# A two-layer attention kernel on one core: the order of score and value runs, of two projections, of some loads and of a few sums is changed

## The chip, the core and the metric

The kernel runs on one core of a Trainium2 chip. A core has five engines with a queue of instructions each: TensorE (in the profile PE, its weight loads PEld), which multiplies matrices and writes to PSUM; VectorE (DVE); ScalarE (ACT); GpSimd (POOL); and SyncE (SP), which here only issues DMA transfers, as GpSimd does too. Each queue is worked in the order written; engines wait for each other by semaphores. SBUF holds the working data, PSUM the sums of the matmuls, in eight banks of 128 x 512 float32. The metric is the device time of one execution in microseconds; lower is better.

## The reference

All is float32. The input x is 8 x 512 x 32 x 32: 8 batches of 512 channels and 1024 positions (tokens).

Layer 0, for each batch: a layer norm over the 512 channels of each token, then `q`, `k`, `v` = xn @ W.T + b, split into 8 heads of 64 channels; `softmax(q k^T / 8) v` in each head; then

```python
out = out @ Wo.T + bo + residual
```

where `residual` is x itself.

Layer 1, for each batch, on the result: a group norm (32 groups of 16 channels), `q`, `k`, `v` from three 512 x 512 matrices, one head of 512 channels:

```python
logits = jnp.einsum('bcn,bcm->bnm', q, k) * scale
attn = jax.nn.softmax(logits, axis=-1)
o = jnp.einsum('bnm,bcm->bcn', attn, v)
out = jnp.einsum('oc,bcn->bon', wp, o) + bp[None, :, None]
return x + out.reshape(B, C, H, W)
```

## The kernel before

**Work per batch.** `fast_path` takes the batches one after the other and both layers of a batch together. (A second path, for scores that overflow, is compiled but not entered.) For a batch: values and queries of layer 0; attention of layer 0; the key projection of the next batch's layer 0, first unit; output projection with residual; group norm, with the second unit of the keys beside it; layer 1 (query-key product `qa` with wq and wk multiplied into one matrix, scores, values with wv and wp multiplied into one, output). The order of TensorE, VectorE, ScalarE and GpSimd is the order in which the Python code emits the instructions (`manual_schedule`), SP's order too.

**Seven products.** Every 512 x 512 by 512 x 1024 product is done on 2 x 2 blocks with seven block products in place of eight. `STEPS` lists them: two operands, one of three PSUM sums `x`, `y`, `z`, and whether the sum is opened or continued. Block sums of the weights are called S1 to S4, those of the data T1 to T4 (`add_operand`, VectorE, 128 x 1024 each). A `Product` is half of such a multiplication (a unit, r = 0 or 1). `step` emits one block product (four full-array matmul records of 512 columns) and then the work due with it: a copy of the sum out of PSUM (`copy`, by a `shift` function that adds bias or residual) and additions into the result (`out`). After step 4 the block (1,1) is formed from `x` and `y`; step 6 continues `y` and so waits until VectorE has read it.

**Side work.** `later` puts small pieces on a list; `tick` emits one, once per step of a product and once per key chunk of the values; `until` empties the list as far as needed. Layer norm of a later batch (`LayerNorm.queue`), operand sums and the softmax sums are spread over the TensorE work in this way.

**Attention of layer 0.** A `Pair` is two heads (128 channels) against half of the queries (512); there are 8 pairs a batch, i = 0 to 7. `scores` makes 8 tiles, one for each 128 keys: the two heads' matmuls use 64 rows of the array each and run side by side into the two banks of one wide PSUM tile (`wide_psum`, pool of three), ScalarE takes the exp of the whole tile into SBUF (`p`), and VectorE adds the tiles up into `sum`. `values` multiplies with the values, each head in 64 columns of the array, into one single bank (`bank`, pool of two), and ScalarE copies that to `o`. The loop runs one pair ahead: scores 0, rest of the queries, scores 1, values 0, scores 2, values 1, ... scores 7, values 6, values 7. A float32 matmul of the code appears as two records in the profile, so scores of a pair are 32 records in 16 steps of two.

**Softmax sums.** Two pairs make a `PairSums`. After a pair's scores GpSimd's DMA queue halves and folds `sum` (lines 529, 533); VectorE then transposes, reduces and inverts it (`invert_folded`, `invert_sums`, lines 537 to 538 and 774 to 778), ScalarE makes eight small copies (line 864), VectorE spreads them (line 523) and scales `o` (line 873). The inverse is emitted at tile m = 4 of a later score run in the first half of a batch, and as side work in the second. In the last batch the last two pairs are summed by matmuls with ones instead (`product`, tile `den`).

**Residual.** In the output projection (`project_out`) the `shift` function issues the DMA for the residual `xr` when the sum is ready to be copied, and VectorE adds it (line 889). `x1_away`, `w_a`, `w_m` are other DMAs of that stage in SP's queue.

**The opening.** Weights are loaded, wq and wk (and wv and wp) of layer 1 multiplied into one, layer norm of batch 0 done in pieces (`norm(n)` emits n of them). `complete("k", wk_now)` emits the key weights' block sums on GpSimd (line 218) and stores them for later batches (line 211).

**Pools.** SBUF tiles of 128 x 1024 come from a pool of 46, those of 128 x 512 from a pool of 9. A tile that takes a slot waits for the last reader of the slot's previous tile.

The loop that the change turns around:

```python
next_scores()
q_last.rest()
for i in range(HEADS):
    p = pairs[i]
    if i + 1 < HEADS:
        next_scores()
    ...
    p.values(scaled=(i == HEADS - 1 and not more))
```

Of the kernel before, what the change touches and what calls it, by code (L numbers as in the profile page):

```python
# [15 lines left out]
ALU = mybir.AluOpType  # L16
# [4 lines left out]
P = 128  # L21
# [40 lines left out]
]  # L62
BLOCK_OF = {1: (0, 0), 4: (1, 1), 5: (1, 0), 6: (0, 1)}
SLOTS = ["11", "12", "22", "S1", "S2", "S3", "S4"]


@with_exitstack
def fast_path(ctx: ExitStack, tc: tile.TileContext, x: bass.AP, vecs: dict, weights: dict, out: bass.AP,
# [174 lines left out]

    def complete(n, w):

        sums_of_blocks(nc.gpsimd, w)
        save_w(n, w)

    def complete_later(n, w):
# [4 lines left out]

    wk_now, wv_now = first_w("k"), first_w("v")
    wo = first_w("o")
    wq_now = first_w("q")
    nc.sync.dma_start(out=bq1_row, in_=vecs["bq1"].rearrange("(a c) -> a c", a=1).to_broadcast((P, C)))
# [70 lines left out]
    class Product:  # L329
# [4 lines left out]
        def __init__(self, tag, a, b, part, shift, dest, banks, after=None):  # L334
            self.tag, self.a, self.b, self.part, self.shift, self.dest = tag, a, b, part, shift, dest
            self.banks = banks
            self.after = after or (lambda i, k: None)
            self.behind = []
            self.ahead = None
            self.in_place = False  # L340
            self.pieces = 1
            self.at_once = False
            self.led = []
            self.last = None
            self.done = 0
# [7 lines left out]
        def copy(self, which):  # L353
            u = half_tile(f"u{which}_{self.tag}")
            self.shift(u, self.x, which)
            return u
# [12 lines left out]
        def step(self, n=1):  # L369
            for _ in range(n):  # L370
# [4 lines left out]
                self.open(to, opens)  # L375
                if self.ahead and i + 1 in BLOCK_OF:
                    self.ahead(*BLOCK_OF[i + 1])
                if i in self.led:
# [133 lines left out]
    def add_operands(b):  # L512
        later(*(lambda n=n: add_operand(b, n) for n in ("T1", "T2", "T3", "T4")))

# [266 lines left out]
    class Pair:  # L781


        def __init__(self, b, hf, c, qt, kt, vt, ot):
            self.tag = f"{b}_{hf}_{c}"
            self.hf, self.c, self.vt = hf, c, vt
            self.q = qt[c // 2, hf][:, c % 2, :]
            self.k = [kt[c // 2, k][:, c % 2, :] for k in range(NH)]
            self.p = {}
            self.sum = self.rden = None  # L790
            if c % 2 == 0:
                ot[c // 2, hf] = block(f"o_{self.tag}")
            self.o = ot[c // 2, hf][:, c % 2, :]

        def scores(self, ms):
            for m in ms:
                s = wide_psum(f"s_{self.tag}_{m}")
                for i in range(2):
                    r = slice(i * D, (i + 1) * D)
                    nc.tensor.matmul(s[:, ts(i, HB)], self.k[m // 4][r, ts(m % 4, P)], self.q[r, :],  # L800
                                     start=True, stop=True)
                p = big_tile(f"p_{self.tag}_{m}")
                nc.scalar.activation(p, s, AF.Exp, scale=1.0 / float(D) ** 0.5)  # L803
                self.p[m] = p
# [9 lines left out]
        def values(self, scaled):  # L814
            acc = bank(f"acc_{self.tag}")
            for m in range(NM):
# [10 lines left out]
    class PairSums:  # L827
# [23 lines left out]
        def product(self):  # L851

            self.den = bank(f"den_{self.tag}")
            for k in range(4):
# [20 lines left out]
    def project_out(b, w, ot, stats):  # L875
# [4 lines left out]
        def unit(r):  # L880
            def dest(i, k):
                return x1[i, k][:, r, :]

            def shift(u, ps, which):
                i, k = which
                oc = 2 * i + r
                xr = half_tile(f"xr_{b}_{k}_{oc}")
                nc.sync.dma_start(out=xr, in_=x[b, ts(oc, P), ts(k, HB)])
                nc.vector.scalar_tensor_tensor(u, ps, bo[:, oc : oc + 1], xr, ALU.add, ALU.add)

            def after(i, k):
                later(lambda: nc.vector.bn_stats(stats[:, 2 * i + r, k, :], dest(i, k)))

            return Product(f"out_{b}_{r}", w, ot, channel_part(r), make_shift(shift, True), dest,
                           banks_of(f"out_{b}", r, shared, own="x"), after)
        return [unit(r) for r in range(2)], x1


    class Whole:
# [96 lines left out]
        def values(self, v):  # L996
# [4 lines left out]
            def unit(r):  # L1001
# [6 lines left out]

                def ahead(i, k):
                    if u.last and (i, k) == (0, 1):  # L1010
                        return
                    xr = xr_of[i, k] = half_tile(f"x1r_{b}_{k}_{2 * i + r}")
                    nc.sync.dma_start(out=xr, in_=self.x1[i, k][:, ts(r, HB)])
# [59 lines left out]
    with tc.manual_schedule(engines=ORDERED):  # L1073
# [9 lines left out]

        complete("k", wk_now)
        norm(5)
# [8 lines left out]
        bm_columns.rows(lambda c: [(slice(0, C), wp[c])])  # L1094
        product(wa, nq, nk, "a", 1)
        bm_columns.columns()
        norm(100)
        for k in range(NH):
            for j in range(2):
# [14 lines left out]

        for n, w in (("v", wv_now), ("q", wq_now), ("o", wo), ("a", wa), ("m", wm)):
            complete_later(n, w)
# [7 lines left out]

        def next_values_and_queries(b, wv, wq, ln):

            units, v = project_v(f"v{b}", wv, hb)
            if b == 0:
# [3 lines left out]
            for u in units:  # L1132
                u.rest()
            units, q = project(f"q{b}", wq, bias_of("bq0"), hb, True)
            for u in units:
                u.pieces = 1 if b else 2
            units[0].step(1)
            if ln:
                ln.waiting = False
            units[0].rest()  # L1140
            return v, q, units[1]

        vts, qt, q_last = next_values_and_queries(0, wv_now, wq_now, ln)
        for b in range(B):
# [12 lines left out]

            next_scores()
            q_last.rest()
            for i in range(HEADS):  # L1160
                p = pairs[i]
                if i + 1 < HEADS:
                    next_scores()
                if i < 2 and more:
# [6 lines left out]
                if i == 7 and more:  # L1171
                    hb = operands(ln.result())
                    add_operands(hb)
                p.values(scaled=(i == HEADS - 1 and not more))
                sums = groups[i // 2]
# [3 lines left out]
                elif i % 2 == 1 and sums.folded:  # L1179
# [4 lines left out]
                    else:  # L1184
                        later(nothing, nothing, sums.invert_folded)
                    later(sums.copies, *(lambda s=sums, f=f, n=n: f(s, n) for f in (PairSums.rows, PairSums.scale)
                                         for n in range(2)))
            if more:
                k_units, kn = project(f"k{b + 1}", wk_next, bias_of("bk0"), hb, True)
                k_units[0].rest()  # L1190
            ob = operands(ot)
            o_units, x1 = project_out(b, wo_now, ob, stats)
            o_units[0].step(1)
# [59 lines left out]
            if more:  # L1253
                wv_next = load_w("v", b + 1)
            o_units = whole.values(vm)
# [15 lines left out]
            if more:  # L1271
                wq_next = load_w("q", b + 1)
            if more:
                kt = {ik: block(f"k{b + 1}_again_{ik[0]}{ik[1]}") for ik in kn_away}
                for ik, d in kn_away.items():
                    nc.sync.dma_start(out=wide(kt[ik]), in_=d)
                vts, qt, q_last = next_values_and_queries(b + 1, wv_next, wq_next, ln)

# [383 lines left out]
```

## Time and profile before

| | us |
|---|---|
| median of three runs | 2914.44 |
| lowest and highest run | 2912.37, 2914.49 |
| the profiled execution, time | 2912.76 |
| the profiled execution, span | 2911.0 |

| engine | busy, us | share of the span |
|---|---|---|
| PE | 2889.0 | 99% |
| PEld | 1373.0 | 47% |
| DVE | 1794.9 | 62% |
| ACT | 1055.5 | 36% |
| POOL | 352.7 | 12% |

The granted clock of TensorE is 0.999 of full speed over the span. The lines below show, for a group of equal instructions: start in us from the span's start, time from the first one's start to the last one's end, engine, line of the code, operation, tiles written and read, shape, count, and in brackets how long the engine was idle before and what ended that. Where matmuls follow each other, their recorded lengths overlap (0.59 us each, 0.43 apart), so stretches of TensorE are read from start to start. A line of the chain shows start, length and what ran.

### The profile page before, as it was taken

The page shows a single profiled execution, that of the slowest core. Times are in us where ns is not written, and L with a number is a line of the kernel's source. Part 1 is how long each engine was busy: PE and PEld are TensorE (multiplying, and loading weights), DVE is VectorE, ACT ScalarE, POOL GpSimd, SP SyncE. Part 2 cuts the span into 40 slices and gives each one's busy share as a digit, 9 for nine tenths or more (in the row PEclk, how much of TensorE's full clock was granted, in tenths as well). Part 3 has the DMA queues.
Part 4 walks back from the last instruction along what each step waited for, and adds up shares of the span by engine and source line. Part 5 has one row for each costly group of instructions (what it writes and reads, how often), then busy time and mean ns, then how long its engine had stood idle before and what let it go on. Part 6 is the DMA issues. An engine that isn't in the chain of part 4 may idle for free.

```text
span 2911.0 us, 27160 instructions
## 1 busy us (share of the span) xinstructions
PE 2889.0 (99%) x9695; PEld 1373.0 (47%) x9695; DVE 1794.9 (62%) x2320; ACT 1055.5 (36%) x1724; POOL 352.7 (12%) x511
## 2 busy tenths in 40 slices
PE   9999999999999999999999999999999999999999
PEld 4534455345543455434553345533455334553345
DVE  6677465774657655676556765577556675537744
ACT  3462314612156122651226412264223632126221
POOL 3020011200112011120111201021010210002000
PEclk9999999999999999999999999999999999999999
DMA  8124153341623326233252333423243331412302
GB/s 303 59 62 144 37 152 83 63 145 36 179 52 63 141 54 170 48 65 134 66 158 51 69 127 85 140 55 77 115 119 105 64 112 71 127 32 61 110 8 66
DMA packets 110127, 277.15 MB, mean 95 GB/s; under 512 B 16304, under 2 KB 20704, under 8 KB 109984
## 3 DMA queue, kind: packets, MB, share of 16 engines
q1 hardware_dynamic: 81760, 204.51, 20.2%
q0 software_dynamic: 28128, 70.81, 13.1%
q8 instruction: 78, 1.28, 0.2%
q14 instruction: 65, 0.53, 0.1%
q10 hardware_dynamic: 96, 0.02, 0.0%
HBM read 168.85 MB, written 59.24 MB: 78 GB/s over the span
## 4 chain that ended last, share of the span: by engine, by line
PE 96%; DVE 2%; DMA 1%; issue 0%; ACT 0%; SPq 0%; DVEq 0%; ACTq 0%
PE s L800 15%; PE acc L818 15%; PE x_o L456 6%; PE x_s L448 6%; PE y_s L448 4%; PE z_s L448 4%; PE z_o L456 4%; PE y_o L456 4%; PE x_k L431 3%; PE x_q L431 3%; PE x_v L440 3%; PE x_vm L440 3%; PE x_qa L431 3%; PE x_out L431 2%; PE y_k L431 2%; PE z_qa L431 2%
## 5 line engine op out<-in xcount | busy, mean ns | idle before, releaser
L803 ACT ACTIVATE p<-s 128x1024 f32<-128x1024 f32 x512 | 476.0, 1052 | 76.8 <-PE s L800 76.8
L809 DVE TENSOR_TENSOR sum<-sum,p 128x1024 f32<-128x1024 f32 x384 | 470.3, 1225 | 39.8 <-DVE sum L809 1.4
L818 PE MATMUL acc<-p,v 128*64 128x512 f32 x2048 | 452.0, 595 | 1.3 <-ACT o L822 1.3
L800 PE MATMUL s<-q,k_again 64*128 64x512 f32 x1792 | 399.7, 596 | 0.0
L818 PEld LDWEIGHTS acc<-p,v 128*64 128x64 f32 x2048 | 142.0, 137 | 304.5 <-issue 297.0
L800 PEld LDWEIGHTS s<-q,k_again 64*128 64x128 f32 x1792 | 166.3, 185 | 231.7 <-issue 114.7
L533 POOL DMA_DIRECT2D sum<-sum x78 | 62.6, 806 | 1748.8 <-PE z_vm L440 892.4
L529 POOL DMA_DIRECT2D fold<-sum x312 | 207.4, 750 | 315.1 <-DMA sum<-sum 143.1
L807 DVE TENSOR_TENSOR sum<-p,p 128x1024 f32<-128x1024 f32 x64 | 78.4, 1225 | 200.2 <-ACT p L803 200.2
L448 PE MATMUL x_s<-S_qa,T_gn 128*128 128x512 f32 x256 | 120.3, 592 | 0.0
L456 PE MATMUL x_o<-T_p,S_vm 128*128 128x512 f32 x256 | 115.2, 592 | 0.0
L822 ACT COPY o<-acc 128x512 f32<-128x512 f32 x63 | 36.9, 586 | 210.1 <-PE acc L818 209.9
L928 ACT ACTIVATE p<-p 128x512 f32<-128x512 f32 x128 | 80.7, 630 | 73.1 <-DVE p L350 73.1
L350 DVE TENSOR_TENSOR p<-u(1, 1)_s,y_s 128x512 f32<-128x512 f32 x32 | 22.0, 688 | 132.4 <-ACT u(1, 1)_s L461 132.4
L478 ACT ACTIVATE u(0, 0)_k<-x_k,vecs 128x512 f32<-128x512 f32 x16 | 11.0, 688 | 214.3 <-PE x_k L431 156.8
L864 ACT COPY rr<-r 32x16 f32<-32x16 f32 x256 | 51.6, 202 | 72.9 <-DVE r L774 69.3
L448 PEld LDWEIGHTS x_s<-S_qa,T_gn 128*128 128x128 f32 x256 | 48.6, 190 | 61.2 <-issue 61.2
L456 PEld LDWEIGHTS x_o<-T_p,S_vm 128*128 128x128 f32 x256 | 48.6, 190 | 60.7 <-issue 59.3
L350 DVE TENSOR_TENSOR y<-u(1, 1)_o,y_o 128x512 f32<-128x512 f32 x16 | 11.0, 688 | 99.0 <-ACT u(1, 1)_o L461 99.0
L523 DVE STREAM_TRANSPOSE rden<-rr 128x512 f32<-128x512 f32 (+1 forms) x72 | 53.3, 758 | 26.5 <-ACT rr L864 13.3
L350 DVE TENSOR_TENSOR qa<-u(1, 1)_qa,y_qa 128x512 f32<-128x512 f32 x16 | 11.0, 687 | 81.5 <-ACT u(1, 1)_qa L478 81.5
L440 PE MATMUL x_vm<-w_m,T_gn 128*128 128x256 f32 x256 | 60.5, 379 | 0.0
(356 smaller groups left out, 4588.7 us busy)
## 6 DMA issues: line engine op xcount, KB each, us to landing
sum<-sum POOLq DMA_DIRECT2D x78, 256.0 KB, 3.4
fold<-sum POOLq DMA_DIRECT2D x312, 64.0 KB, 2.4
x<-in_x_dram SPq DMA_DIRECT2D x32, 512.0 KB, 6.6
xr<-in_x_dram SPq DMA_DIRECT2D x64, 256.0 KB, 4.1
x_away<-x SPq DMA_DIRECT2D x32, 512.0 KB
x1r<-x_away SPq DMA_DIRECT2D x63, 256.0 KB, 3.0
k_away<-k SPq DMA_DIRECT2D x28, 512.0 KB, 2.6
k_again<-k_away SPq DMA_DIRECT2D x28, 512.0 KB, 5.6
```

Of the source, the lines that this page charges most:

```text
L431: nc.tensor.matmul(dst, a[:, k, ts(r, P)], b[:, k, :], start=(opens and k == 0), stop=(k == 1), skip_group_check=True)
L440: nc.tensor.matmul(dst[:, ts(m, CB)], b[:, k, ts(2 * r + m, P)], a[:, k, :], start=(opens and m == 0 and k == 0), stop=(k == 1), skip_grou ...
L448: nc.tensor.matmul(dst, b[:, k, ts(r, P)], a[:, k, :], start=(opens and k == 0), stop=(k == 1), skip_group_check=True)
L456: nc.tensor.matmul(dst, a[:, m, ts(r, P)], b[m // 2][:, m % 2, :], start=(opens and m == 0), stop=(m == NM // 2 - 1), skip_group_check=True)
L529: nc.gpsimd.dma_start(out=f[ts(q + i, BL), :], in_=t[ts(n, BL), ts(i, HB)], accum_op=ALU.add if n else ALU.bypass)
L533: nc.gpsimd.dma_start(out=t[:D, :], in_=t[D:, :], accum_op=ALU.add)
L800: nc.tensor.matmul(s[:, ts(i, HB)], self.k[m // 4][r, ts(m % 4, P)], self.q[r, :], start=True, stop=True)
L803: nc.scalar.activation(p, s, AF.Exp, scale=1.0 / float(D) ** 0.5)
L807: nc.vector.tensor_add(self.sum, self.p[0], p)
L809: nc.vector.tensor_add(self.sum, self.sum, p)
L818: nc.tensor.matmul(acc[i * D : (i + 1) * D, :], value_of(self.vt, m, self.c * P + i * D, D), self.p[m][:, ts(i, HB)], start=(m == 0), stop ...
L928: nc.scalar.activation(dest(i, k), dest(i, k), AF.Exp, scale=float(C) ** -0.5)
```

## The change

Six edits, quoted in their core below.

1. The attention loop emits the scores of two pairs in a row and then the values of both: scores 0, scores 1, values 0, values 1, scores 2, scores 3, and so on.
2. In such a run of 16 tiles, tiles 7, 11 and 15 take two single banks instead of one wide PSUM tile, and their exp is two instructions of 512 columns instead of one of 1024. The values' accumulator `acc` and `den` take (half of) a wide tile instead of a single bank.
3. `next_values_and_queries` becomes `next_queries_and_values`: queries come first, both units, with their PSUM sums shared between the units; values second. The weights are loaded in that order, in the opening too.
4. The residual is loaded straight into the tile that the sum is added to, some steps ahead: block (0,0) of both units when the projection is set up, before the next batch's keys; (0,1) at step 0, (1,1) at step 2, (1,0) at step 3 (`LOADS_AT`). `ahead` hooks are called with the step's number.
5. The key weights' block sums of the opening go from GpSimd to VectorE, behind the last layer-norm sum and the variance matmuls; the store of them goes to the end of the layer norm, and the `bm` columns come after the variance matmuls.
6. The first operand sum of the output projection (T1) is emitted as side work in the key projection, in the place of one `nothing`.

```diff
+LOADS_AT = {0: [(0, 0), (0, 1)], 2: [(1, 1)], 3: [(1, 0)]}
...
-    wk_now, wv_now = first_w("k"), first_w("v")
+    wk_now, wq_now = first_w("k"), first_w("q")
     wo = first_w("o")
-    wq_now = first_w("q")
+    wv_now = first_w("v")
...
         def copy(self, which):
-            u = half_tile(f"u{which}_{self.tag}")
+            u = self.loaded.pop(which) if which in self.loaded else half_tile(f"u{which}_{self.tag}")
             self.shift(u, self.x, which)
...
         def scores(self, ms):
             for m in ms:
-                s = wide_psum(f"s_{self.tag}_{m}")
+                if m + self.c % 2 * NM in (7, 11, 15):
+                    s = None
+                    parts = [bank(f"s{i}_{self.tag}_{m}") for i in range(2)]
+                else:
+                    s = wide_psum(f"s_{self.tag}_{m}")
+                    parts = [s[:, ts(i, HB)] for i in range(2)]
...
-                nc.scalar.activation(p, s, AF.Exp, scale=1.0 / float(D) ** 0.5)
+                for dst, src in zip((p[:, ts(i, HB)] for i in range(2)), parts) if s is None else ((p, s),):
+                    nc.scalar.activation(dst, src, AF.Exp, scale=1.0 / float(D) ** 0.5)
...
-            acc = bank(f"acc_{self.tag}")
+            acc = wide_psum(f"acc_{self.tag}")[:, :HB]
...
-            self.den = bank(f"den_{self.tag}")
+            self.den = wide_psum(f"den_{self.tag}")[:, :HB]
...
-            def shift(u, ps, which):
+            def load(which):
                 i, k = which
-                oc = 2 * i + r
-                xr = half_tile(f"xr_{b}_{k}_{oc}")
-                nc.sync.dma_start(out=xr, in_=x[b, ts(oc, P), ts(k, HB)])
-                nc.vector.scalar_tensor_tensor(u, ps, bo[:, oc : oc + 1], xr, ALU.add, ALU.add)
+                xr = u.loaded[which] = half_tile(f"xr_{b}_{k}_{2 * i + r}")
+                nc.sync.dma_start(out=xr, in_=x[b, ts(2 * i + r, P), ts(k, HB)])
+
+            def ahead(n):
+                for which in LOADS_AT.get(n, []):
+                    if which not in u.loaded:
+                        load(which)
+
+            def shift(t, ps, which):
+                oc = 2 * which[0] + r
+                nc.vector.scalar_tensor_tensor(t, ps, bo[:, oc : oc + 1], t, ALU.add, ALU.add)
...
+            u.ahead = ahead
+            load((0, 0))
+            return u
...
-        complete("k", wk_now)
         norm(5)
...
         product(wa, nq, nk, "a", 1)
+        norm(3)
+        sums_of_blocks(nc.vector, wk_now)
+        norm(1)
         bm_columns.columns()
         norm(100)
+        save_w("k", wk_now)
...
-        def next_values_and_queries(b, wv, wq, ln):
-
-            units, v = project_v(f"v{b}", wv, hb)
+        def next_queries_and_values(b, wq, wv, ln):
+
+            units, q = project(f"q{b}", wq, bias_of("bq0"), hb)
...
-            units, q = project(f"q{b}", wq, bias_of("bq0"), hb, True)
+            units, v = project_v(f"v{b}", wv, hb)
...
-            units[0].rest()
-            return v, q, units[1]
+            for u in units:
+                u.rest()
+            return q, v
...
-            next_scores()
-            q_last.rest()
             for i in range(HEADS):
+                if i % 2 == 0:
+                    for _ in range(2):
+                        next_scores()
                 p = pairs[i]
-                if i + 1 < HEADS:
-                    next_scores()
...
+                if i == 7:
+                    ob = operands(ot)
...
-                        later(nothing, nothing, sums.invert_folded)
+                        later(lambda: add_operand(ob, "T1"), nothing, sums.invert_folded)
...
+            o_units, x1 = project_out(b, wo_now, ob, stats)
             if more:
                 k_units, kn = project(f"k{b + 1}", wk_next, bias_of("bk0"), hb, True)
                 k_units[0].rest()
-            ob = operands(ot)
-            o_units, x1 = project_out(b, wo_now, ob, stats)
...
-                wv_next = load_w("v", b + 1)
+                wq_next = load_w("q", b + 1)
...
-                wq_next = load_w("q", b + 1)
-            if more:
+                wv_next = load_w("v", b + 1)
```

## The prediction

> **What bounds the kernel now.** I read the page first (shares, chain), then TensorE's timeline in the attention of layer 0, then the engines that feed it, then the three other places that the diff touches.
>
> ```profile
> span 2911.0 us, 27160 instructions
> PE 2889.0 (99%) x9695; PEld 1373.0 (47%) x9695; DVE 1794.9 (62%) x2320; ACT 1055.5 (36%) x1724; POOL 352.7 (12%) x511
> PE 96%; DVE 2%; DMA 1%; issue 0%; ACT 0%; SPq 0%; DVEq 0%; ACTq 0%
> ```
>
> TensorE is never without work: the span can only shrink where its steps are longer than they must be. From the chain in order of time (start, length), then from TensorE's timeline:
>
> ```profile
> 573.73 7.07 PE s L800 x32
> 580.80 13.88 PE acc L818 x64
> ```
> ```profile
> 2667.46 7.09 PE L818 MATMUL acc<-p,v 128*64 128x512 f32 x32
> 2674.48 7.14 PE L800 MATMUL s<-q,k_again 64*128 64x512 f32 x32
> 2681.55 7.09 PE L818 MATMUL acc<-p,v 128*64 128x512 f32 x32
> ...
> 476.88 1.98 PE L431 MATMUL x_q<-x,w_q 128*128 128x512 f32 x4
> 478.70 1.88 PE L431 MATMUL z_q<-x,w_q 128*128 128x512 f32 x4
> 480.42 1.88 PE L431 MATMUL x_q<-T_h,w_q 128*128 128x512 f32 x4
> ```
>
> Read starts, not lengths. Four full-array steps take 480.42-478.70 = 1.72 us, 0.429 each. A run of scores or values is 16 such steps, two half-array matmuls side by side in each: 6.87. The run of scores takes 2681.55-2674.48 = 7.07, so 0.20 too long; the run of values 7.02, 0.15 too long; two runs of values without scores between take 13.88, only 0.14 too long together. So the loss is paid when the array's shape changes (64*128, 128*64, 128*128), and in the second step after. x_q, which follows scores, shows it too: 1.82 from its start to z_q's in place of 1.72.
>
> The engines that follow the scores, ScalarE then VectorE, in one run of eight tiles:
>
> ```profile
> 2703.83 7.44 ACT L803 ACTIVATE p<-s 128x1024 f32<-128x1024 f32 x8 [0.47 <-PE s L800]
> 31.64 1.07 ACT L281 COPY w_a_first<-psw_a 128x512 f32<-128x512 f32 x2 [1.06 <-PE psw_a L278]
> 2705.80 1.22 DVE L807 TENSOR_TENSOR sum<-p,p 128x1024 f32<-128x1024 f32 x1 [4.88 <-ACT p L803]
> 2707.13 7.87 DVE L809 TENSOR_TENSOR sum<-sum,p 128x1024 f32<-128x1024 f32 x6
> ```
>
> The other places: the residual in the output projection, the opening's sums on GpSimd, and the next batch's key projection.
>
> ```profile
> 1683.86 0.75 DVE L889 SCALAR_TENSOR_TENSOR u(1, 1)_out<-x_out,bo,xr 128x512 f32<-128x512 f32 x1 [2.58 <-DMA xr<-in_x_dram]
> 1685.39 1.98 PE L431 MATMUL y_out<-o,w_o 128*128 128x512 f32 x4 [0.53 <-DVE x L350]
> ```
> ```profile
> 15.35 1.23 DVE L578 TENSOR_TENSOR lns<-x,x 128x1024 f32<-128x1024 f32 x1 [14.08 <-DMA x<-in_x_dram]
> 26.59 7.68 POOL L218 TENSOR_TENSOR w_k_first<-w_k_first,w_k_first 128x512 f32<-128x512 f32 x4 [24.25 <-DMA w_k_first<-in_L_conv_Wk_dram]
> 26.97 2.30 DVE L578 TENSOR_TENSOR lnq<-sq,sq 128x1024 f32<-128x1024 f32 x1
> 34.88 1.07 PE L573 MATMUL var<-lnq,ones_c 128*64 128x512 f32 x2 [1.50 <-DVE lnq L582]
> ```
> ```profile
> 600.82 1.71 ACT L864 COPY rr<-r 32x16 f32<-32x16 f32 x8
> 603.50 0.69 ACT L478 ACTIVATE u(1, 1)_k<-x_k,vecs 128x512 f32<-128x512 f32 x1 [0.97 <-PE x_k L431]
> 605.01 1.93 PE L431 MATMUL y_k<-x,w_k 128*128 128x512 f32 x4
> ```
>
> **The change part by part.**
>
> *Runs of two pairs, queries before values.* A batch now has 8 runs of scores and 7 of values (6 single, one double); it will have 4 and 4. Over 8 batches: 32 x 0.20 = 6.4 us and 24 x 0.15 = 3.6 us less. The second half of the queries no longer stands between two runs of scores: its own slow step (0.10) goes 8 times, and one entry into scores out of it (523 ns where 429 is normal, 16 now, 8 then from values) goes 8 times: 0.8 + 0.8. Sum -11.6 us. Below: if the slow second step of scores (0.104) belonged to the pair and not to the run, 3.3 of it would stay.
>
> *Does ScalarE keep up with 16 tiles in a row?* TensorE makes a tile every 0.859. Eight exps take 7.44, one alone 1.05, so one every (7.44-1.05)/7 = 0.913: 0.054 slower. Three wide buffers: tile n waits for the exp of tile n-3. Measured from the start of the run, exp n ends at 2.20 + 0.917n (the first starts at 2703.83-2702.65 = 1.18 and takes 1.02), and a tile's first matmul can follow 0.16 after that. Tile 7 at present: wants 6.11, may start at 2.20+4x0.917+0.16 = 6.03. Sixteen in three buffers would run out: tile 15 wants 12.99 and could start at 13.36, a stall of 0.37. With tiles 7, 11 and 15 in single banks a wide tile waits for the exp four back. Their exps become two of half size; two copies of that size take 1.07, one 0.585, so 0.485 each, 0.97 a pair. Then tile 8 has 0.9 us in hand, tile 12 0.7, tile 15 0.4, and the values' accumulator (now a wide buffer, freed by exp 12) 0.5. I take no stall. Upper bound: halves that don't overlap at all, 0.69 each (L478's length); the three pairs cost 1.4 more and the run ends 0.38 late, 32 x 0.38 = 12 us.
> [...]
>
> *Buffers.* The slots that the 16 exps write were last read by the values of the group before or by folding DMAs issued 20 us and more earlier, so no wait there: 0.
>
> *VectorE gets further behind.* Its first add comes 3.15 after the run's start; 7 adds take 1.33+7.87 = 9.2, so the second pair's sum ends at 21.55, where the group is 27.8 long. That is 2.3 us later before the group's end than now. Inside a batch the slack of about 4 us covers it (sums' inverses 1.9, rows and scaling 2.7). At the last group it meets the key projection: there the four operand sums T_h (L510) and the moved first operand sum of the outputs (1.22) come ahead of the inverse. T_h now ends at 596.08, then at 598.4; with 1.22 and the key addition's 0.6 behind it the inverse starts at 600.25, now 599.02. The eight small copies that follow it (600.82, ending 602.53) then end near 603.8, and behind them on ScalarE the PSUM copy u(1,1), now at 603.50, waits. So y_k waits 0.3 longer, 7 times: +2.1 us. Bounds: 0 (the slack is larger), and 0.9 a batch, 6 us, if the fold's DMAs also come late.
>
> *Residual loaded sooner.* Per output unit y_out waits for x(1,1). In single starts the step z_out to y_out is 0.44 in eight of 16 cases; in seven it is longer by 0.04 to 0.68, 2.2 us together, where VectorE waited for the xr DMA (1683.86 shows 2.58 of waiting); the last one (1.23) waits for group norm's work. The new loads can start some 8 steps of 1.72, 14 us, ahead of their use, in slots that are free by then; landing takes 4.1 (median). They go through SP ahead of x1_away and w_a, needed later still. -2.2 us; bounds 0 and -3.
>
> *Opening.* GpSimd's four sums (7.68) stretch VectorE's adds from 1.23 to 2.30 and 0.69 to 1.65, and var waits for them 1.66 in its starts. Moved to VectorE behind those adds, the four cost 4 x 0.65 = 2.6 while TensorE does var (1.9) and goes on to psw_m; the transpose after them comes at about 33.5, now 35.99. -1.6 us; bounds -0.5 (the four adds hold up the transpose; 14 us of psw_m hide most of that) and -2.4 (ps_columns' 0.8 fills a wait too). SP's new order of weights (q before v) is hidden: all are issued by 31, first used after 74.
>
> *Last batch.* Its last values waited 1.28 for the copy that frees a bank; the wide buffer ends that, but den now waits some 0.6 for the late second sum: -0.7, bounds -1.3 and +2.
>
> Sum: -11.6 + 0 + 2.1 - 2.2 - 1.6 - 0.7 = -14.0 us. The profiled execution took 2912.76 (span 2911.0 and 1.8 around it), so 2898.8 beside it. The three runs are 2912.37 to 2914.49 with median 2914.44, 1.7 above the profiled one; I add 1.2 of that: **2900 us**.
>
> **Rivals.** A: ScalarE falls short by the upper bound, so waits of 0.2 to 0.38 a group take the place of the shape changes: 6 to 12 us back, 2906 to 2912. Against it: the 0.4 in hand above. B: the change doesn't do what it says, the slow steps belong to each pair: then only 2.2+1.6+0.7-2.1 = 2.4 and the queries' 1.6 remain, 2910. Against it: 13.88 for two pairs of values in a row. C, slower: the two matmuls of a split tile write different tiles and wait for different exps, so they may run one after the other instead of side by side. Each split tile then takes 1.72 instead of 0.86: 96 x 0.86 = 83 us, 2983. 16 parted tiles of the 96 undo the gain, 23 make it slower by over 0.2%. For it: no row has such a tile. Against it: in the wide tile, too, the halves lie in two banks.
>
> **How the numbers follow.** Forecast 0.78, A 0.12, B 0.05, C 0.05. A measurement here tells about 0.2% (5.8 us) from no change: faster means below 2908.6. The forecast alone runs from 2894 (terms at their good ends: -11.6-3-2.4-1.3) to 2907 (6 us of key waits, 1 less from the residual). The range 2893 to 2910 takes in most of A and B. Faster: forecast and half of A, 0.84; same: half of A and B, 0.11; slower: C, 0.05.
>
> **What would show it.** Runs of 64 score matmuls that take 13.94 from start to start, then 13.88 for values; no idle of the weight load before acc behind an exp; sum ending 21.5 after the run's start; y_out after z_out at 0.44 fifteen times; var without a wait; y_k behind the copies rr by some tenths. Wrong if s steps beyond the eighth stretch above 0.43, if a split tile's second matmul starts 0.4 after its first, or if y_k waits over 1 us.

## The result, and the profile after

The changed kernel took **2895.03 us** (median of four runs, 2894.74 to 2895.12), the kernel before 2913.73 us beside it: a ratio of 0.9936, 95% interval 0.9919 to 0.9953, or 18.7 us less. The profiled execution moved from 2912.76 to 2894.74 us, 18.0 us, where the prediction had 14.0. From the page of the changed kernel:

```profile
span 2892.7 us, 27272 instructions
PE 2874.9 (99%) x9695; PEld 1380.2 (48%) x9695; DVE 1789.6 (62%) x2324; ACT 1058.0 (37%) x1820; POOL 345.5 (12%) x507
PE 98%; DVE 1%; DMA 0%; ACT 0%; issue 0%; DVEq 0%; SPq 0%; ACTq 0%
```

TensorE has the same 9695 matmuls and is still the bound: its share of the chain rose from 96% to 98%. What changed is how long its steps stand apart. TensorE's timeline in the last batch's attention (start, length):

```profile
2664.91 13.95 PE L822 MATMUL acc<-p,v 128*64 128x512 f32 x64
2678.79 14.00 PE L804 MATMUL s<-q,k_again 64*128 64x512 f32 x64
2692.73 7.09 PE L822 MATMUL acc<-p,v 128*64 128x512 f32 x32
```

A run of 64 score matmuls takes 2692.73 - 2678.79 = 13.94 us from start to start, and the values of two pairs 2678.79 - 2664.91 = 13.88: both to the hundredth as forecast. In the records of that run the two matmuls of a step start 7 ns apart, in parted tiles as in wide ones, and no step after the second stands more than 0.43 us behind the one before. One sign reads otherwise at first: the profile puts idle time of the weight load ahead of acc, up to 0.8 us, down to an exp, 32 times. But the exp that frees acc's buffer, tile 12's, ended at 2692.12, 0.6 us ahead of that load, so the load did not wait for it; and scores to values is 0.52 us in both kernels. ScalarE and VectorE over the same run:

```profile
2679.97 14.96 ACT L807 ACTIVATE p<-s 128x1024 f32<-128x1024 f32 x19 [0.45 <-PE s L804]
2692.38 7.87 DVE L813 TENSOR_TENSOR sum<-sum,p 128x1024 f32<-128x1024 f32 x6
```

Nineteen exps (13 wide ones and six halves) end at 2694.93, 2.2 us after the run, and no matmul is late for them. Lengths grow along the run (a wide one from 1.02 to 1.21 us), so starts have to be read here too: wide exps start 0.904 us apart, halves 0.477 (medians over the whole execution). The second sum ends with the last of the six additions at 2692.38 + 7.87 = 2700.25, 21.5 us after the run's start.

Sums of starts, by place: each step's distance from the step before it, less its nominal 0.429 us, added over the execution (in us).

| place | before | after | number before, after |
|---|---|---|---|
| second step of scores | 6.64 | 3.32 | 64, 32 |
| scores to values | 5.39 | 3.08 | 56, 32 |
| values to scores | 4.77 | 2.39 | 48, 24 |
| second step of values | 2.87 | 1.66 | 57, 33 |
| projections to scores | 1.49 | 0.76 | 16, 8 |
| into x_q out of scores, and its second step | 1.71 | 0.10 | 17, 1 |
| z_out to y_out | 3.16 | 0.98 | 16, 16 |

The price of each shape change is what it was; there are about half as many.

### The profile page after: what moved, and what is told of

Read it like the earlier page. It is cut to its first block, busy times and chain, and to the rows that moved or that the text cites. A ratio compares the mean times of both kernels' runs of the same rounds, so it can differ in the third digit from the quotient of the medians.

```text
span 2892.7 us, 27272 instructions
## 1 busy us (share of the span) xinstructions
PE 2874.9 (99%) x9695; PEld 1380.2 (48%) x9695; DVE 1789.6 (62%) x2324; ACT 1058.0 (37%) x1820; POOL 345.5 (12%) x507
## 4 chain that ended last, share of the span: by engine, by line
PE 98%; DVE 1%; DMA 0%; ACT 0%; issue 0%; DVEq 0%; SPq 0%; ACTq 0%
PE s L804 15%; PE acc L822 15%; PE x_o L453 6%; PE x_s L445 6%; PE y_s L445 4%; PE z_o L453 4%; PE z_s L445 4%; PE y_o L453 4%; PE x_qa L428 3%; PE x_v L437 3%; PE x_vm L437 3%; PE x_q L428 3%; PE x_out L428 3%; PE x_k L428 3%; PE z_qa L428 2%; PE y_q L428 2%
## 5 line engine op out<-in xcount | busy, mean ns | idle before, releaser
L807 ACT ACTIVATE p<-s 128x1024 f32<-128x1024 f32 (+1 forms) x608 | 478.8, 984 | 42.7 <-PE s L804 42.7
L804 PE MATMUL s<-q,k_again 64*128 64x512 f32 x1792 | 392.1, 592 | 0.0
L900 DVE SCALAR_TENSOR_TENSOR xr<-x_out,bo,xr 128x512 f32<-128x512 f32 x64 | 47.7, 745 | 38.5 <-PE x_out L428 38.5
```

The lines of the kernel that those rows point to most:

```text
L804: nc.tensor.matmul(parts[i], self.k[m // 4][r, ts(m % 4, P)], self.q[r, :], start=True, stop=True)
L807: nc.scalar.activation(dst, src, AF.Exp, scale=1.0 / float(D) ** 0.5)
```

## Is the price paid by the run or by the pair?

**One part undone.** In the changed kernel the order is put back to one pair of scores ahead of the values.

```diff
+            next_scores()
             for i in range(HEADS):
-                if i % 2 == 0:
-                    for _ in range(2):
-                        next_scores()
                 p = pairs[i]
+                if i + 1 < HEADS:
+                    next_scores()
```

> The changed kernel with one edit undone: scores of one pair in a row again, one pair ahead of the values, as before the change; queries first, parted tiles, wide accumulators, residual loads and opening stay changed. A batch then has 7 runs of scores and 7 of values in place of 4 and 4. Theory (the price belongs to the run, that is to each change of the array's shape, 0.20 us for an entry into scores and 0.15 us for one into values): 24 x 0.20 + 24 x 0.15 = 8.4 us more than the changed kernel, 2903.4 us; steps above 0.429 us grow only at the run borders and in the second step of a run. Rival B (slow steps belong to each pair): 2895 us. A second rival (the gain comes from VectorE's and ScalarE's order, not from the array): the borders stay at 0.10 + 0.10 us but their number does not explain the difference.

2902.95 us, 0.997 of the kernel before (0.9958 to 0.9982), 7.9 more than the changed kernel. In the sums of starts the four places rise by 2.50 (second step of scores), 2.31, 2.39 and 1.21: 8.4 us for 24 + 24 runs more. So this one edit is worth some 8 of the 18.7 us, and the number of runs explains it. Rival B falls, and so does the rival that the gain lies in VectorE's and ScalarE's order.

**The price multiplied.** The kernel before, with its runs cut in halves for six pairs of a batch: the same matmuls in twice as many runs.

```diff
-        def values(self, scaled):
+        def values(self, scaled, between=None):
             acc = bank(f"acc_{self.tag}")
             for m in range(NM):
+                if m == NM // 2 and between:
+                    between()
...
                 if i + 1 < HEADS:
-                    next_scores()
+                    next_scores(slice(0, NM // 2 if i < 6 else NM))
```

> The kernel before with its runs cut in halves: scores of four tiles, then values of four tiles, in turn, for the scores of pairs 1 to 6 and the values of pairs 0 to 5 of each batch; the inverse of a group's sums is taken up one tile sooner so that it still stands ahead of its copies. That adds 6 runs of scores and 6 of values a batch, 48 and 48, with the same number of pairs, tiles and matmuls. Theory (price per run): 48 x 0.20 + 48 x 0.15 = 16.8 us more than the kernel before, 2930.5 us. Rival B (price per pair): no change, 2913.7 us. Rival (price per entry only, second steps free when a run is short): 48 x 0.20 = 9.6 us, 2923 us.

2958.42 us, 46.2 more than the 2912.19 of the kernel before beside it. That is neither 16.8 nor 0. TensorE's timeline in a second half of scores, and ScalarE's there:

```profile
2694.36 2.85 PE L800 MATMUL s<-q,k_again 64*128 64x512 f32 x12
2698.64 1.13 PE L800 MATMUL s<-q,k_again 64*128 64x512 f32 x4 [1.44 <-ACT p L803]
```
```profile
2695.83 1.70 ACT L866 COPY rr<-r 32x16 f32<-32x16 f32 x8 [3.75 <-DVE r L774]
2697.56 3.78 ACT L803 ACTIVATE p<-s 128x1024 f32<-128x1024 f32 x4
```

The copies of the inverted sums now come ahead of the second half's exps on ScalarE and wait there for VectorE; the exps behind them wait too, and the fourth tile of scores has no buffer. By starts, sixteen such steps cost 27.2 us, and 1.7 more in the steps behind them. The run borders (the first two steps of each run) cost 16.8 more than in the kernel before. So the edit had added a wait of its own, and it was taken out: the copies were put four steps of values later.

```diff
+                    if i < HEADS // 2:
+                        later(*(nothing,) * (NM // 2))
                     later(sums.copies, *(lambda s=sums, f=f, n=n: f(s, n) for f in (PairSums.rows, PairSums.scale)
```

> The kernel before with its runs cut in halves, as in the run of that name, and with the copies of the inverted sums put four steps of values later for the first two groups of a batch, so that on ScalarE they stand behind the second half's exps and not ahead of them. In the run with the halves, 16 stalls of about 1.66 us stood behind those copies (28 us with the long step after each); they should be gone. Theory (price per run): 48 entries into scores and 48 into values at 0.20 and 0.15 us, 16.8 us more than the kernel before, 2930 us. Rival B (price per pair): 2913.5 us. Rival (the stall has another cause): 2958 us again.

2929.2 us beside 2912.29: 16.9 more, ratio 1.0059 (1.0046 to 1.0073); no step of scores beyond the second is long, and the run borders again cost 16.8 more by starts. The price belongs to the run. Rival B falls here too.

## Do the parted tiles do anything?

```diff
-                if m + self.c % 2 * NM in (7, 11, 15):
+                if m + self.c % 2 * NM in ():
```

> The changed kernel with no parted tiles: all 16 score tiles of a run of two pairs go to the three wide buffers, one exp each. Theory (an exp every 0.917 us against a tile every 0.859 us, tile n waits for the exp three back): tile 15 may start at 13.36 us instead of 12.99, so a run of 64 score matmuls takes 14.31 us instead of 13.94: 32 x 0.37 = 11.9 us more than the changed kernel, 2907 us, and the steps beyond the ninth tile run at the exps' pace. Rival (ScalarE has more in hand than its rows say, or queues absorb it): 2895 us. Rival (the exps' pace sets all tiles of a run from the third on): 13 x 0.058 = 0.75 us a run, 24 us, 2919 us.

2907.98 us, 0.9985 of the kernel before (0.9976 to 0.9994): 12.9 more than the changed kernel. Two of TensorE's lines, then the weight load's waits for the exp in this kernel and in the changed one (total, times, longest):

```profile
2662.67 14.44 PE L804 MATMUL s<-q,k_again 64*128 64x512 f32 x64
2677.04 13.95 PE L822 MATMUL acc<-p,v 128*64 128x512 f32 x64
```
```profile
PEld s L804 <- ACT p L807: 212.6, 416, 0.6
```
```profile
PEld s L804 <- ACT p L807: 67.5, 232, 0.5
```

The run takes 14.37 us here and 13.94 with parted tiles; the first long steps come in the ninth and tenth tile, and from the eleventh on every tile has one of 0.48 to 0.49 in place of 0.43, which is the exps' pace. Over the execution the score steps are 12.5 us longer, 0.39 a run for the 0.37 worked out from the exps' rows. In the changed kernel a weight load still waits for an exp 232 times, but early enough that its matmul is not late. So three wide buffers are short by this much for 16 tiles in a row, and with three tiles parted over the two banks they are not.

The other half of the buffers' edit, undone:

```diff
-            acc = wide_psum(f"acc_{self.tag}")[:, :HB]
+            acc = bank(f"acc_{self.tag}")
...
-            self.den = wide_psum(f"den_{self.tag}")[:, :HB]
+            self.den = bank(f"den_{self.tag}")
```

> The changed kernel with the accumulators of the values, and the sums' product of the last batch, back in the two single banks that the parted tiles now use as well. Theory (buffers come free in the order of their use): the first accumulator of a group takes the bank of the first half of tile 15, whose exp ends about 1.7 us after the run of scores, so values start 1.9 us late: 32 x 1.9 = 60 us more than the changed kernel, 2955 us. Rival (the accumulators' place matters only in the last batch): 1.4 us more, 2896.5 us.

2953.55 us, ratio 1.0143 (1.0128 to 1.0159), 58.5 more than the changed kernel.

```profile
2675.07 14.00 PE L804 MATMUL s<-q,k_again 64*128 64x512 f32 x64
2690.77 13.95 PE L822 MATMUL acc<-p,v 128*64 128x512 f32 x64 [1.70 <-ACT p L807]
```

2690.77 - 2675.07 is 15.70 in place of 13.94: the accumulator waits for an exp in every group, by the order of the buffers that of tile 15's first half. Parting the tiles without moving the accumulator would have made the kernel slower than before.

## The wait that did not come: y_k

The largest miss of the prediction is a term that it added. Behind the last group VectorE's chain is late, as it said, but y_k hardly waits. ScalarE, VectorE and TensorE of the changed kernel at the end of layer 0 in the second batch:

```profile
593.19 0.70 DVE L534 STREAM_TRANSPOSE foldt<-fold 128x512 f32<-128x512 f32 x1
```
```profile
594.99 1.71 ACT L868 COPY rr<-r 32x16 f32<-32x16 f32 x8 [0.96 <-DVE r L771]
596.78 0.69 ACT L475 ACTIVATE u(1, 1)_k<-x_k,vecs 128x512 f32<-128x512 f32 x1
```
```profile
598.29 1.93 PE L428 MATMUL y_k<-x,w_k 128*128 128x512 f32 x4
```

Take times from the start of the key projection, 587.89 here and 594.61 before. The inverse starts at 5.30, 0.89 later than before (4.41); the prediction had 1.23. The copies end at 8.81; u(1,1) starts at 8.89, exactly as before, and y_k at 10.40, exactly as before. The forecast of 0.3 us a batch was a difference between two times of which one was 0.3 too late: it added lengths (2.3 for the lag, then 1.22 for T_o behind the recorded end of T_h) where starts give 2.2 and 1.14, and T_o starts 0.09 ahead of that end. Is there any cover left, or does the term stand at zero by a hair?

```diff
-                        later(lambda: add_operand(ob, "T1"), nothing, sums.invert_folded)
+                        def first_sum():
+                            add_operand(ob, "T1")
+                            nc.vector.tensor_sub(wide(ob["T1"]), wide(ob["12"]), wide(ob["11"]))
+
+                        later(first_sum, nothing, sums.invert_folded)
```

> The changed kernel with the first operand sum of the outputs computed twice (the second time over the first, same values), so that the inverse of the last group's sums starts 1.13 us later on VectorE at the end of layer 0. In the changed kernel the eight small copies end 0.08 us ahead of the time at which ScalarE's u(1, 1) of the key projection could start, and VectorE's addition behind that copy ends 0.1 us ahead of the y_k that it releases. Theory (that 0.1 us is all the cover there, so that the term of +2.1 us in the prediction was right in place and only some tenths too large in each batch): y_k starts about 1.05 us later in 7 batches, 7.4 us more than the changed kernel, 2902.4 us. Rival (y_k does not hang on that chain, or VectorE has slack there): 2895 us.

2904.87 us, 9.8 more. The second subtraction starts 1.25 us behind the first (it writes the same block). The seven steps z_k to y_k stand 8.82 us above nominal, against 0.24 in the changed kernel (one batch alone): 1.16 in five batches, 1.51 in two. So the place was right, the cover is some 0.09 us in those five batches, and the changed kernel stands just short of the wait. TensorE's line says what it hangs on:

```profile
600.96 1.98 PE L428 MATMUL y_k<-x,w_k 128*128 128x512 f32 x4 [0.99 <-DVE k L347]
```

## The residual and the opening, each alone

On the kernel before, the residual's loads alone:

```diff
+            def load(which):
+                i, k = which
+                xr = u.loaded[which] = half_tile(f"xr_{b}_{k}_{2 * i + r}")
+                nc.sync.dma_start(out=xr, in_=x[b, ts(2 * i + r, P), ts(k, HB)])
...
+            u.ahead = ahead
+            load((0, 0))
```

> The kernel before with one part of the change: the residual of layer 0 is loaded steps ahead of its use (the output projection's units are also built ahead of the key projection's, which that needs). Theory (y_out waits for VectorE, VectorE for the load): 2.2 us less in the starts from z_out to y_out, the last batch's 1.23 stays, 2911.5 us where the kernel before takes 2913.7, and no VectorE operation on x_out waits for a transfer. Rival (the loads collide with the weights and the folding transfers on their way): 0 or some us more.

2911.28 us beside 2913.20: 1.9 less, ratio 0.9996 (0.9987 to 1.0005), by itself within what the runs can tell. In the starts z_out to y_out falls from 3.16 to 0.98 us, and every one of the sixteen but the last is 0.440 to 0.443. That agrees with the 2.2 of the prediction. Then the opening's sums alone:

```diff
-        complete("k", wk_now)
...
         product(wa, nq, nk, "a", 1)
+        norm(3)
+        sums_of_blocks(nc.vector, wk_now)
+        norm(1)
         bm_columns.columns()
         norm(100)
+        save_w("k", wk_now)
```

> The kernel before with one part of the change: the four sums of the opening's key weights on VectorE, behind the sums of squares, in place of GpSimd. By the prediction 1.6 us less. By the changed kernel's profile more: there the four var matmuls took 1.01 us together, 3.58 before, because the two halves of the array run side by side when both sums are there and one after the other when the second is late: 2.6 us less, 2911.1 us, and the first x_k starts 2.6 us sooner beside the same landing of x. Rival (VectorE's later chain hangs on the moved sums): under 1 us less.

2909.33 us beside 2913.20: 3.9 less (0.9988, 0.9979 to 0.9997), more than either figure. VectorE's adds, which took 2.30 and 1.65 us beside GpSimd's sums, take 1.22 and 0.69 in the changed kernel. TensorE's lines of the changed kernel:

```profile
23.56 7.13 PE L274 MATMUL psw_a<-nat_k,nat_q 128*128 128x512 f32 x16
30.63 1.08 PE L570 MATMUL var<-lnq,ones_c 128*64 128x512 f32 x4
...
48.40 1.96 PE L428 MATMUL x_k<-x,w_k_first 128*128 128x512 f32 x4
```

Two things were missed. First, var's four matmuls take 1.01 us when both sums are there (they start in pairs, side by side), and 1.0 for each pair when the second sum is late; the prediction had counted 1.9 for all four. Second, the clock. From this psw_a to x_k is 24.84 us here, and 24.83 or 24.84 in all seven executions with the new opening as the change makes it. With the old opening it was 27.28 in the profile of before and 27.26 in another, but 29.18 and 28.92 in the two other executions profiled. The granted clock explains the difference. The kernel with the residual's loads alone, in stretches (busy time of PE, PEld, DVE, ACT, POOL, then PEclk, DMA share, GB/s):

```profile
34.00:35.00 1.00, 0.70 (x2) 0.19 (x2) 0.24 (x1) 0.00 (x0) 1.00 (x3) 0.89 1.04 380
35.00:36.00 1.00, 1.00 (x2) 0.26 (x2) 0.15 (x1) 0.00 (x0) 1.00 (x3) 0.50 1.07 397
36.00:38.00 2.00, 2.00 (x3) 0.92 (x4) 1.26 (x5) 0.54 (x2) 0.51 (x1) 0.50 0.99 303
38.00:39.00 1.00, 1.00 (x3) 0.38 (x2) 0.93 (x5) 0.00 (x0) 0.00 (x0) 0.90 1.08 420
```

TensorE waited 1.75 us for var's second sum, and then ran at half its clock for 3.41 us, which costs 1.7. The profile of before had 1.50 us of waiting there and a clock of 1.00 throughout, so nothing in it showed this. To see whether the idle time does it, the sums were put ahead of the addition that var's second half needs, once and twice:

```diff
-        norm(3)
-        sums_of_blocks(nc.vector, wk_now)
-        norm(1)
+        for _ in range(2):
+            sums_of_blocks(nc.vector, wk_now)
+        norm(4)
```

> The changed kernel with the four sums of the opening's key weights still on VectorE, but ahead of the last addition that the second half of var needs instead of behind it. TensorE then stands idle for about 1.5 us between the two halves of var, and the halves run one after the other. Theory on the idle alone: 2.1 us more than the changed kernel, 2897.1 us, granted clock 1.00 behind the idle. In two of the three profiles with the old opening an idle of 1.75 us and more was followed by a granted clock of 0.50 for about 3.4 us, which cost 1.7 us; in the third, an idle of 1.50 us was not. If 1.5 us suffices here, 2898.8 us.

2897.44 us, 2.4 more than the changed kernel. The wait was 0.57 us, not 1.5, since TensorE came to var later in this execution; the clock stayed at 1.00. So this run says nothing on where the border lies. (Its expectation speaks of 1.75 us and more for both executions that lost their clock; in that of the halved runs it was 1.48.)

> As the run with the sums ahead, with the four sums computed twice (the same values), so that TensorE stands idle for about 4.1 us in the opening. Theory (an idle well above 1.7 us brings the granted clock to 0.50 for about 3.4 us): 4.7 us for the wait and 1.7 us for the clock, 6.4 us more than the changed kernel, 2901.4 us, with matmuls of twice the length behind the wait. Rival (the long matmuls of the old opening came from the transfers and from GpSimd's work beside them, not from the idle): 4.7 us, 2899.7 us, granted clock 1.00.

2903.06 us, 8.0 more. The wait is 3.16 us, and behind it:

```profile
37.00:41.00 4.00, 4.00 (x9) 2.41 (x10) 2.99 (x11) 0.54 (x2) 0.00 (x0) 0.50 1.04 417
41.00:44.00 3.00, 3.00 (x5) 1.17 (x4) 3.00 (x3) 1.90 (x3) 0.00 (x0) 0.56 1.01 399
```

The clock is 0.50 for 6.8 us, twice as long as behind 1.75, and x_k comes 7.6 us later from psw_a. There were no GpSimd sums beside it, and the transfers beside it (DMA share about 1.0) also ran beside the openings that kept their clock, so this speaks for the idle time as the cause. Idle time alone doesn't say when, though: of the four profiles with the old opening two kept their clock (1.50 and 1.47 us of waiting) and two lost it (1.75 and 1.48). The clock's records lie on a grid: in the profiles of before and of the changed kernel every change comes a whole number of 3.4133 us behind the first record, which lies at 9.02 and at 9.19 us (806, 807 and 849 of them before, 801, 802 and 844 after), and the 3.4 and 6.8 us here are one and two of them. Both profiles also show a second place: in the last batch x_qa waits 2.60 and 2.61 us, and behind that the clock is at 0.50 for 3.41 us. Whether a wait's place on the grid decides between 1.47 and 1.48 us was not shown.

## A version that is faster than both

In the changed kernel's profile, y_out's step still stands 0.44 us behind z_out's, 0.012 too long, and its own second matmul comes 0.533 behind the first. The same 0.1 us showed behind the stalls of the halved runs. So here a wait of hundredths costs a tenth in the next step. The records of the weight loads show where the tenth comes from. Where nothing is late, a matmul's load starts 0.427 us ahead of it, together with the matmul before. y_out's load waits for VectorE and starts 0.002 ahead; the next load starts 0.108 behind it, and the second matmul is 0.104 late. y_q's and y_qa's loads start 0.055 ahead, and the second matmul is 0.05 late; y_s's start 0.129 ahead, and nothing is (medians of the changed kernel). A change of shape looks the same: the load starts 0.002 ahead, and the second step is 0.104 late with loads of 128 columns (scores), 0.051 with 64 (values). In the kernel without parted tiles, whose loads wait for an exp 416 times, a tile loses 0.06 from the eleventh on.

The edit reads y out sooner. The quadrant (1,1) is x + y; here the bias or the residual goes onto y, which is complete a step before x, so y's bank is free long before the last step adds to it.

```diff
...
+                elif i == 3 and self.shift.twice:
+                    self.u3 = self.copy((1, 1), self.y)
+                elif i == 4 and self.shift.twice:
+                    self.out(1, 1, self.u3, self.x)
                 elif i == 4:
...
-LOADS_AT = {0: [(0, 0), (0, 1)], 2: [(1, 1)], 3: [(1, 0)]}
+LOADS_AT = {0: [(0, 0), (0, 1)], 1: [(1, 1)], 3: [(1, 0)]}
...
```

> The changed kernel with one more edit, in the projections of keys, queries, outputs and layer 1's first product: the quadrant (1,1) is x + y, and the shift by the bias (or the residual) is now put on y, which is complete a step before x, and x is added to it. So y's bank is read out a step sooner, and the last step, which adds to that bank, waits for nothing; the residual of that quadrant is loaded a step sooner. Theory (the last step waits for the chain of x, copy, addition by some hundredths, and every step behind a wait starts with a matmul 0.05 to 0.10 us too long): the changed kernel's 1.75 (y_out), 1.09 and 0.24 (y_k), 0.81 (y_q), 0.80 (y_qa) and 0.16 of z_out to y_out go, 4.8 us less than the changed kernel, 2890.2 us. Rival (the long matmul belongs to this step's weights or to its going back to an open sum, not to a wait): 0.4 us less, 2894.6 us.

**2891.03 us**, 0.9928 of the kernel before (0.9914 to 0.9941) and 4.0 less than the changed kernel, with no overlap of the runs (2890.13 to 2891.39 against 2894.74 to 2895.12). Steps of y_out are 1.72 us apart on both sides, with 0.429 in each matmul, and its loads start 0.427 ahead. First the changed kernel's two lines, 1.82 apart, then this one's, 1.72 apart:

```profile
613.81 1.98 PE L428 MATMUL y_out<-o,w_o 128*128 128x512 f32 x4
615.63 1.88 PE L428 MATMUL x_out<-T_o,w_o 128*128 128x512 f32 x4
```
```profile
613.95 1.88 PE L432 MATMUL y_out<-o,w_o 128*128 128x512 f32 x4
615.67 1.88 PE L432 MATMUL x_out<-T_o,w_o 128*128 128x512 f32 x4
```

The rival, that the long matmul belongs to the step's weights or to its open sum, falls: weights and sum are the same. The sum of starts falls by 4.1. Of the 4.8 expected, 0.6 of y_k stays where the small matmuls of the group norm come between its steps. The last batch's z_out to y_out gains 0.8 that was not expected, and its first product of layer 1 loses 0.7, where the changed kernel's clock was at 0.50 for 3.41 us; over the span the granted clock was 0.998 in this execution and 0.999 in the changed kernel's.

## Why the prediction was right, and where its sum was off

The mechanism was right and the number within its range, 2900 against 2895.0. Terms beside the profiled execution:

| step | predicted | measured |
|---|---|---|
| shape changes and x_q | -11.6 | -11.6 (the first six rows of the table above) |
| ScalarE's stall | 0 | 0 |
| y_k behind VectorE's lag | +2.1 | +0.2 |
| residual | -2.2 | -2.2 |
| opening | -1.6 | -3.35 |
| last batch (den) | -0.7 | -0.8 |
| not priced | 0 | -0.5 |
| sum | -14.0 | -18.3 |

*Shape changes.* Counted and priced from starts, and the runs confirmed by undoing and by multiplying them. Queries before values, 1.6 of the 11.6, has no run of its own, nor has the moved T1: what that one gains is not known.

*ScalarE.* No stall, as taken. The upper bound, halves that don't overlap, did not come up: 0.477 us for a half, where the prediction took 0.485 from two copies of that size. Without the parted tiles the stall is 0.39 a run, so the model behind the 0.37 holds.

*y_k.* The mis-sized term, 1.9 us. The sentence that failed is "the inverse starts at 600.25": by starts it is 599.9 on that clock. In a chain whose cover is 0.1 us, lengths that overlap by 0.08 each are too rough.

*Opening.* The other one, 1.75 us. 2.4 of the 3.35 are var: "TensorE does var (1.9)" was the wrong step, since side by side it is 1.01. The other 0.9 lies ahead of psw_a, where the executions differ by up to 1.5 us whatever the kernel (23.56 to 25.05 for this start): chance, as far as the profiles tell. Between medians the opening is worth more than 2.4, which fits an old opening that sometimes loses its clock: it then took 1.6 to 1.9 us longer, and the one profile before the prediction had not lost it.

*Last batch.* From den's start to the values it took 2.35 us before and 1.55 after. The wait for the bank went, and a wait of 0.4 for the second sum came in its place (1.17 without it, in the kernel with wide tiles alone).

*Not priced.* z_qa behind x_qa in the last batch starts 0.5 us less late. These steps ran partly at a clock of 0.50 in both profiles, so part of it may be chance.

*Range.* Its ends don't follow from its terms. With 2900 at -14.0, the good ends (-18.3) give 2895.7 and not 2894; key waits of 6 in place of 2.1 and 1 less from the residual give 2905 and not 2907. The measured sum equals that good end, -18.3, but by other terms and in part by luck: y_k near its bound of 0, the residual as forecast, the opening past its bound of -2.4 with 0.9 of chance in it.

*Rivals.* A was decided by the kernel without parted tiles: with 0.39 a run, it is what that kernel does. B fell with the single and the halved runs. C fell with the 7 ns between a parted tile's two matmuls.

## What to carry to other kernels

A shape change of TensorE's tiles has a price in starts (here 0.20 us into scores, 0.15 into values) that can be counted and multiplied, so runs twice as long pay it half as often; but the run's length is bought with buffers, and the two buffer edits that look like details here cost 13 and 58 us when one of them is undone. Where a chain's cover is a tenth of a microsecond, add starts and not lengths, and before trusting one profile's wait, ask what the clock would do behind it in another execution: here it stayed at 1.00 behind 1.47 us and fell to 0.50 behind 1.48.

## What the runs showed of the hardware

Two points were not expected. Behind a weight load that is held back by a wait, and not only behind a change of shape, the second matmul started up to 0.10 us late (0.533 for 0.429 behind a wait of 0.012 in y_out, and behind the stalls of the halved runs; 0.48 where the load still came 0.055 ahead), so reading out one bank a step sooner gained 4 us. And behind waits of 1.48 and 1.75 us TensorE's clock was at 0.50 for 3.4 us, behind one of 3.16 us for 6.8, while behind others of 1.47 and 1.50 us it stayed at 1.00.
